# Dealing the TensorE fetch of a three-layer graph attention out in steps, with more columns in it

## The chip, the cores and the metric

The kernel runs on one core of one Trainium2 chip. The metric is the device time of that core in microseconds (us). A core has five engines with a queue of instructions each: PE (TensorE, matmuls; PEld is its loading of weights), DVE (VectorE), ACT (ScalarE), POOL (GpSimd, which issues the indirect DMAs here) and SP (SyncE, which issues plain DMAs).

## What is computed

A graph of 12500 nodes with 32 features each and 400000 directed edges. Three layers of graph attention follow each other, with 2, 2 and 1 heads; then an edge network, whose input and result are put together with a residual and layer norms. One attention layer, cut to what matters:

```python
def _gat(x, edge_index, W, att_s, att_d, bias, heads, ch, neg_slope):
    h = (x @ W.T).reshape(n, heads, ch)
    a_s = (h * att_s[None]).sum(-1)
    a_d = (h * att_d[None]).sum(-1)
    src, dst = (edge_index[0], edge_index[1])
    logits = jax.nn.leaky_relu(a_s[src] + a_d[dst], neg_slope)
    m = jax.ops.segment_max(logits, dst, num_segments=n)
    ex = jnp.exp(logits - m[dst])
    denom = jax.ops.segment_sum(ex, dst, num_segments=n)
    alpha = ex / (denom[dst] + 1e-16)
    out = jax.ops.segment_sum(alpha[:, :, None] * h[src], dst, num_segments=n)
    return out.reshape(n, heads * ch) + bias
```

So every edge needs the row `h[src]` and the number `a_s[src]` of its source node (32 + heads numbers), and then a softmax and a sum over the edges that share a destination. The edge network takes, per edge, the source's row, the destination's row and 32 features of the edge through two small matrices, and takes the maximum over each destination's edges.

## The kernel before

**Tiling.** The edges come sorted by destination. Each of the 128 partitions holds 3125 consecutive edges, one edge per column. A layer walks over the columns in chunks of 60: 50 full chunks and four shorter ones (48, 32, 29 and 16 columns), 54 in all. Layer 2 walks backwards. Sums and maxima over a destination's edges are scans along the columns, with the running values handed from chunk to chunk and at the end from partition to partition. All loops are unrolled, and a scheduler puts each engine's instructions in the order of the program; every engine then works through its own list in order and waits on semaphores for the others.

**Two ways to a source row.** The function `rows_of(c)` allocates a buffer `g` of the pool `gpool` (3 buffers) for a chunk and fills it, column by column. Most columns are filled by a gather: one indirect DMA (L71, issued on POOL) that fetches 128 rows, one for each partition, from the node table in device memory. Every seventh column (`EVERY`, L90; those with t % 7 == 6, so 446 of a layer's 3125, eight or nine of a chunk's 60) is fetched by TensorE instead. For this the whole node table lies in SBUF as `by_group`, three bf16 pieces of each number (so that their sum is the fp32 number), 7 blocks of 14 groups of nodes. `Fetch.fetch` (L244) does, for a chunk: `bm` (L251), a mask on DVE which of the 14 groups a column's nodes are in, for all the chunk's columns at once; then for each column

- `ones_of` spreads the places of the 128 nodes over the partitions with a matmul into PSUM (`places_p`, L255; fp32, two records in the profile), and DVE compares them with the partition numbers (`oh`, L258): seven one-hot matrices of 128x128;
- 21 matmuls (7 blocks, 3 pieces, L270) with these as weights, summed in the PSUM tile `acc` (two buffers);
- DVE multiplies `acc` with `bm` (`mine`, L273) and sums over the 14 groups into the column of `g` (L275).

The one-hot matrix of the next column is made ahead of the matmuls of this one.

**A chunk.** At the head of chunk c the loop of `attention` calls `rows_of(c + 1)`: the gathers and the whole fetch of the next chunk stand in program order ahead of all operations of chunk c. These are then:

- DVE: masks, logits `lg` (up to L804), running maximum (L810), the differences (L815 to L818); ACT: exponentials `wt` (L820), kept in PSUM;
- for each head: ACT `rx` (L830), DVE the rows of `g` times `wt` (`gf`, L833, the last reader of `g`: the second one of a chunk, in layer 3 the only one, frees the buffer), ACT L835, and three scans on DVE (L839; five in layer 3);
- ACT copies `rows` (L842) and SP stores them (L844);
- layers 1 and 2: `finish` divides (`divided`, L586 to L593), applies the activation on ACT (L602 to L604), and in four blocks of up to 16 columns transposes (L615, L617), multiplies with the next layer's weights on PE (L620, L621) and transposes back (L623, L624); layer 3: `finish3` divides, adds the residual (L647) and does a layer norm (L633 to L641);
- SP stores what the next layer reads (L849, L853).

The PSUM tile `fixed` is one bank that holds several things at a time: `places_p`, `small_p` (`wt` and the denominators), biases. Accesses to it from different engines wait for each other.

At the start of layers 2 and 3 `node_groups` builds `by_group` from the layer's node table, with 98 gathers of its own.

In layer 1 every fourth chunk also issues a tenth of the clearing of the table `x_e` (`clear`, from the tile `zeros`) on SP's queue.

## Time and profile before

| what | value |
|---|---|
| median of 10 runs | 22407.24 us (22397.67 to 22432.04) |
| the profiled execution | 22416.65 us, span 22414.9 us |
| mean granted clock of TensorE | 0.696 of full speed |
| busy: PE, PEld, DVE, ACT, POOL | 43%, 20%, 44%, 13%, 50% of the span |
| DMA | 881.63 MB, mean 39 GB/s |
| chain of waits that ended last | "another core or an unknown queue" 34%, DVE 25%, PE 23%, issue 10% |
| attention layer 1 (first to last L842) | about 624 to 6137 us |
| attention layer 2 | about 6573 to 12095 us |
| attention layer 3 | about 12531 to 17508 us |
| edge network | from about 17.5 ms to the end |

The costliest groups of instructions, from the page and the table of lines:

| line | engine | count | busy us | mean ns | idle before, us |
|---|---|---|---|---|---|
| L270 the 21 matmuls of a column | PE | 28098 | 6630.9 | 393 | 671.1 |
| L71 gathers, layer 1 | POOL | 2679 | 2537.6 | 947 | 3181.4, mostly for L833 |
| L71 gathers, layer 2 | POOL | 2679 | 2545.9 | 950 | 3156.8, mostly for L833 |
| L71 gathers, layer 3 | POOL | 2679 | 2542.4 | 949 | 2649.7, mostly for L833 |
| L258 one-hot | DVE | 1338 | 1447.9 | 1082 | 225.1 |
| L273 select | DVE | 1338 | 874.9 | 654 | 5542.2 |
| L275 sum into `g` | DVE | 1338 | 850.0 | 635 | 0.1 |
| L255 spread | PE | 2676 | 666.3 | 337 | 4044.5 |
| L839 scans | DVE | 918 | 757.4 | 869 | 5.5 |
| L833 rows times weights | DVE | 270 | 604.7 | 2240 | 4.0 |

How to read it: busy time is the sum of the durations of a group; "idle before" is how long the engine stood ahead of the group's instructions, which is a wait only if something else waits for that engine. A line is that of the kernel before. Group means mix several shapes where a line has several. "Remote" as the end of a wait names no instruction of this core. A matmul's end is modelled in the profile.

### The profile page before, as it was taken

Reading aid. Unit: us, or ns where it says so; the run is one execution under the profiler, and the core shown is the slowest. Engines: PE = TensorE matmul, PEld = TensorE weight load, DVE = VectorE, ACT = ScalarE, POOL = GpSimd, SP = SyncE. Lnnn points to the kernel's source line nnn. Section 1 sums busy time; section 2 is a strip of 40 time slices with the busy share of each in tenths; the row PEclk is TensorE's granted clock in tenths of the full one; section 3 lists DMA queues with packets and bytes.
Section 4 is the critical chain, followed back from the end, with each engine's and each line's share of the span. In section 5 each row is a group of like instructions: output and inputs, shape, how many; then the busy total and the mean of one; then the engine's idle time right before and its main releaser. Section 6 shows DMA issues by size and latency. Waiting matters only on the chain.

```text
span 22414.9 us, 107898 instructions
## 1 busy us (share of the span) xinstructions
PE 9721.3 (43%) x35914; PEld 4506.4 (20%) x35914; DVE 9825.7 (44%) x13987; ACT 2922.1 (13%) x3898; POOL 11205.9 (50%) x11780
## 2 busy tenths in 40 slices
PE   0545555554534444444443344444444233334332
PEld 0222222222212222222221122222222111111111
DVE  2444444444524444444443344444444445555554
ACT  0111111111101111111111000101001111111111
POOL 6444444444354444444445544445444666666663
PEclk5777777777767777777776676776767666666666
DMA  3111111111101111111111111111111111111111
GB/s 50 45 38 38 49 38 38 40 39 30 34 17 28 28 28 28 30 28 28 28 30 31 31 38 40 42 36 42 38 40 41 45 48 59 55 59 55 59 55 43
DMA packets 562458, 881.63 MB, mean 39 GB/s; under 512 B 267998, under 2 KB 482493, under 8 KB 548445
## 3 DMA queue, kind: packets, MB, share of 16 engines
q1 hardware_dynamic: 185036, 665.01, 8.3%
q0 software_dynamic: 376544, 206.39, 6.4%
q8 instruction: 285, 4.67, 0.1%
q10 hardware_dynamic: 304, 3.20, 0.0%
q14 instruction: 289, 2.37, 0.0%
HBM read 370.51 MB, written 503.27 MB: 39 GB/s over the span
## 4 chain that ended last, share of the span: by engine, by line
another core or an unknown queue 34%; DVE 25%; PE 23%; issue 10%; ACT 4%; POOL 3%; DMA 1%; DVEq 0%; SPq 0%; POOLq 0%; ACTq 0%
PE acc L270 15%; PE ph L981 3%; DVE gf L833 3%; DVE gf L839 3%; DVE oh L258 2%; PE pv L987 1%; DVE yt L617 1%; DVE mine L273 1%; PE ph L620 1%; DVE y L589 1%; PE fixed L255 1%; PE pa L621 1%; DVE y L593 1%; DVE z L908 1%
## 5 line engine op out<-in xcount | busy, mean ns | idle before, releaser
L270 PE MATMUL acc<-by_group,oh 128*128 128x504 bf16 (+2 forms) x28098 | 6630.9, 393 | 671.1 <-issue 663.1
L71 POOL DMA_INDIRECT g<-table,src_i x2679 | 2537.6, 947 | 3181.4 <-DVE gf L833 2355.2
L71 POOL DMA_INDIRECT g<-table,src_last x2679 | 2545.9, 950 | 3156.8 <-DVE gf L833 2355.4
L71 POOL DMA_INDIRECT g<-table,src_first x2679 | 2542.4, 949 | 2649.7 <-DVE gf L833 1847.5
L71 POOL DMA_INDIRECT xs<-table,src_last x3125 | 2985.0, 955 | 1566.1 <-issue 944.2
L270 PEld LDWEIGHTS <-oh 128*128 128x128 bf16 x28098 | 2940.5, 105 | 4070.9 <-issue 1729.8
L273 DVE TENSOR_TENSOR mine<-acc,bm 128x504 f32<-128x504 f32 (+2 forms) x1338 | 874.9, 654 | 5542.2 <-remote 3419.3
L255 PE MATMUL fixed<-ident,fat 128*128 128x128 f32 x2676 | 666.3, 337 | 4044.5 <-DVE oh L258 1493.8
L620 PE MATMUL ph<-yt,w_bd 128*128 128x512 f32 (+2 forms) x840 | 615.0, 824 | 4125.6 <-issue 2793.8
L258 DVE TENSOR_TENSOR oh<-fixed,kid 128x896 bf16<-128x896 f32 x1338 | 1447.9, 1082 | 225.1 <-remote 108.2
L981 PE MATMUL ph<-xt,wb_bd 128*128 128x512 f32 (+2 forms) x832 | 504.4, 693 | 2303.4 <-DVE xt L974 1696.2
L623 DVE STREAM_TRANSPOSE tb<-ph 128x512 f32<-128x512 f32 (+2 forms) x420 | 284.8, 678 | 2704.4 <-remote 2144.7
L255 PEld LDWEIGHTS fixed<-ident,fat 128*128 128x128 f32 x2676 | 554.0, 224 | 4381.8 <-issue 2629.2
L620 PEld LDWEIGHTS ph<-yt,w_bd 128*128 128x128 f32 x840 | 179.8, 250 | 4268.0 <-issue 3809.3
L275 DVE TENSOR_REDUCE g<-mine 128x36 f32<-128x504 f32 (+2 forms) x1338 | 850.0, 635 | 0.1
L987 PE MATMUL pv<-ht,w_bd 128*128 128x512 f32 (+2 forms) x832 | 517.7, 723 | 725.3 <-ACT ht L983 534.0
L820 ACT ACTIVATE fixed<-lg 128x120 f32<-128x120 f32 (+3 forms) x162 | 41.2, 254 | 5636.4 <-DVE oh L258 5635.9
L839 DVE TENSOR_TENSOR_SCAN gf<-rx,gf 128x488 f32<-128x488 f32 (+4 forms) x918 | 757.4, 869 | 5.5
L621 PE MATMUL pa<-yt,a_bd 128*128 128x512 f32 (+2 forms) x840 | 599.0, 805 | 323.5 <-DVE at L624 248.6
L842 ACT COPY rows<-gf 128x2040 f32<-128x2040 f32 (+3 forms) x162 | 628.6, 3880 | 560.4 <-DVE gf L839 560.4
L981 PEld LDWEIGHTS ph<-xt,wb_bd 128*128 128x128 f32 x832 | 187.6, 233 | 2549.1 <-DVE xt L974 1697.3
L625 ACT COPY tb<-at 128x32 f32<-128x32 f32 (+4 forms) x420 | 92.4, 220 | 4468.6 <-DVE at L624 3933.0
(333 smaller groups left out, 10853.1 us busy)
## 6 DMA issues: line engine op xcount, KB each, us to landing
sums<-rows SPq DMA_DIRECT2D x100, 1080.0 KB
table<-tb SPq DMA_DIRECT2D x50, 1020.0 KB
sums<-rows SPq DMA_DIRECT2D x50, 1020.0 KB
x_e<-zeros SPq DMA_DIRECT2D x10, 5000.0 KB
xs<-table,src_last POOLq DMA_INDIRECT x3125
table<-tb SPq DMA_DIRECT2D x50, 990.0 KB
xr<-x_e SPq DMA_DIRECT2D x50, 960.0 KB
table<-xr SPq DMA_DIRECT2D x50, 960.0 KB
```

Of the source, the lines that this page charges most:

```text
L71: return nc.gpsimd.indirect_dma_start(out=dst, out_offset=None, in_=table, in_offset=bass.IndirectOffsetOnAxis(ap=idx, axis=0))
L255: nc.tensor.matmul(places_p, lhsT=bcast(self.at[:, i0 + m:i0 + m + 1], [P, P]), rhs=ident, start=True, stop=True)
L258: nc.vector.tensor_tensor(oh, bcast(places_p[:, None, :], [P, KT, P]), bcast(kid[:, :, None], [P, KT, P]), op=ALU.is_equal)
L270: nc.tensor.matmul(acc, lhsT=oh[:, k, :], rhs=by_group[:, i, k, :KN * w], start=(k == i == 0), stop=(k == KT - 1 and i == 2))
L273: nc.vector.tensor_mul(mine, acc.rearrange("p (w b) -> p w b", b=KN), bcast(bm[:, m:m + 1, :], [P, w, KN]))
L275: nc.vector.tensor_reduce(g[:, t - t0, :w], mine, axis=AX.X, op=ALU.add)
L620: nc.tensor.matmul(ph, lhsT=w_bd, rhs=yt, start=True, stop=True)
L621: nc.tensor.matmul(pa, lhsT=a_bd, rhs=yt, start=True, stop=True)
L833: nc.vector.tensor_mul(v[:, h * wd:h * wd + ch, cur].rearrange("p f t -> p t f"), g[:, :, h * ch:(h + 1) * ch], bcast(wt[:, h, :, None], [ ...
L839: nc.vector.tensor_tensor_scan(turned(gf[:, o:o + k], rev), turned(rx[:, :k], rev), turned(gf[:, o:o + k], rev), 0.0, op0=ALU.mult, op1=AL ...
L981: nc.tensor.matmul(ph, lhsT=wb_bd[:, s, h, :], rhs=x, start=(s == 1), stop=(s == 0))
L987: nc.tensor.matmul(pv, lhsT=w2_bd[:, h, :], rhs=hts[h], start=(h == 0), stop=(h == 1))
```

## The change

`EVERY` becomes 6, 6 and 5 in place of 7, 7 and 7: 520, 520 and 625 columns of a layer are fetched by TensorE, and as many fewer gathered. `Fetch.fetch` becomes `Fetch.columns`, which returns a `Paced` object: a generator that emits one column's instructions at each step, and a rule that spreads the steps evenly over a given number of points. `rows_of(c + 1)` still emits its gathers at the head of chunk c; the columns are emitted at `step()` calls between the operations of chunk c: after the logits, after `wt`, after L835 and after the scans of each head, and in `finish` after the activation and in each block after the matmuls (11 points in a full chunk of layers 1 and 2, for 10 columns and 11 steps), in `finish3` at five places (9 points in layer 3, for 12 columns and 13 steps). What is left is emitted at the head of the next chunk (`rest`). Within the fetch the select of a column (L273, L275) now comes after the matmuls of the next. The mask `bm` has room for 12 columns in place of 9, and the tile `zeros`, from which `clear` writes, has 250 numbers per partition in place of 500, with more and smaller packets for the same bytes.

```diff
--- before.py
+++ after.py
@@ -87,7 +87,7 @@
 
-    EVERY = {1: 7, 2: 7, 3: 7}
+    EVERY = {1: 6, 2: 6, 3: 5}
...
@@ -146,7 +146,7 @@
-    zeros = const.tile([P, 500], F32, name="zeros")
+    zeros = const.tile([P, 250], F32, name="zeros")
...
@@ -218,6 +218,29 @@
+    class Paced:
+
+
+        def __init__(self, steps, count):
+            self.steps, self.count, self.taken, self.passed = steps, count, 0, 0
+
+        def at_points(self, points):
+            self.points = points
+            return self
+
+        def __call__(self):
+            self.passed += 1
+            while self.taken < min(self.count, -(-self.count * self.passed // self.points)):
+                next(self.steps)
+                self.taken += 1
+
+        def rest(self):
+            for _ in self.steps:
+                pass
+
+    def alone():
+        pass
+
     class Fetch:
 
 
@@ -241,15 +264,14 @@
         def __contains__(self, t):
             return bool(self.every) and t < TE // self.every * self.every and t % self.every == self.every - 1
 
-        def fetch(self, psum, g, t0, n, bufs=2):
+        def columns(self, psum, g, t0, n):
+
+
 
             todo = [t for t in range(t0, t0 + n) if t in self]
             if not todo:
-                return
+                return Paced(iter(()), 0)
             pool, w, i0 = self.pool, self.w, todo[0] // self.every
-            bm = pool.tile([P, 9, KN], F32, name="bm")[:, :len(todo), :]
-            nc.vector.tensor_tensor(bm, bcast(count[:, None, :KN], [P, len(todo), KN]),
-                                    bcast(self.b[:, i0:i0 + len(todo), None], [P, len(todo), KN]), op=ALU.is_equal)
 
             def ones_of(m):
                 nc.tensor.matmul(places_p, lhsT=bcast(self.at[:, i0 + m:i0 + m + 1], [P, P]), rhs=ident,
@@ -259,20 +281,32 @@
                                         bcast(kid[:, :, None], [P, KT, P]), op=ALU.is_equal)
                 return oh
 
-            coming = ones_of(0)
-            for m, t in enumerate(todo):
-                oh = coming
-                if m + 1 < len(todo):
-                    coming = ones_of(m + 1)
-                acc = psum.tile([P, 512], F32, name="acc", bufs=bufs)[:, :KN * w]
-                for k in range(KT):
-                    for i in range(3):
-                        nc.tensor.matmul(acc, lhsT=oh[:, k, :], rhs=by_group[:, i, k, :KN * w],
-                                         start=(k == i == 0), stop=(k == KT - 1 and i == 2))
+            def select(m, acc, bm):
                 mine = pool.tile([P, D + 4, KN], F32, name="mine")[:, :w, :]
                 nc.vector.tensor_mul(mine, acc.rearrange("p (w b) -> p w b", b=KN),
                                      bcast(bm[:, m:m + 1, :], [P, w, KN]))
-                nc.vector.tensor_reduce(g[:, t - t0, :w], mine, axis=AX.X, op=ALU.add)
+                nc.vector.tensor_reduce(g[:, todo[m] - t0, :w], mine, axis=AX.X, op=ALU.add)
+
+            def steps():
+                bm = pool.tile([P, 12, KN], F32, name="bm")[:, :len(todo), :]
+                nc.vector.tensor_tensor(bm, bcast(count[:, None, :KN], [P, len(todo), KN]),
+                                        bcast(self.b[:, i0:i0 + len(todo), None], [P, len(todo), KN]), op=ALU.is_equal)
+                oh, acc = ones_of(0), None
+                for m in range(len(todo)):
+                    coming = ones_of(m + 1) if m + 1 < len(todo) else None
+                    done, acc = acc, psum.tile([P, 512], F32, name="acc", bufs=2)[:, :KN * w]
+                    for k in range(KT):
+                        for i in range(3):
+                            nc.tensor.matmul(acc, lhsT=oh[:, k, :], rhs=by_group[:, i, k, :KN * w],
+                                             start=(k == i == 0), stop=(k == KT - 1 and i == 2))
+                    if m:
+                        select(m - 1, done, bm)
+                    oh = coming
+                    yield
+                select(len(todo) - 1, acc, bm)
+                yield
+
+            return Paced(steps(), len(todo) + 1)
 
     def node_groups(li, idx, w):
 
@@ -298,7 +332,7 @@
     def clear(table, part=0, parts=1):
...
         k = TE * table.shape[1] // parts
-        z = next(z for z in range(500, 0, -1) if k % z == 0)
+        z = next(z for z in range(250, 0, -1) if k % z == 0)
...
@@ -592,7 +626,7 @@
         bias = b_all[:, 2, :] if li == 3 else biases[li]
         nc.vector.tensor_add(y, y, bcast(bias[:, :, None], [P, D, n]))
 
-    def finish(li, pool, psum, den, v, n):
+    def finish(li, pool, psum, den, v, n, step=alone):
 
         y = pool.tile([P, D * T], F32, name="y", bufs=1)[:, :D * n].rearrange("p (f t) -> p f t", t=n)
         divided(li, y, den, v, n)
@@ -602,6 +636,7 @@
         nc.scalar.activation(e, y, AF.Relu, scale=down)
         nc.scalar.activation(y, y, AF.Relu, scale=up)
         nc.scalar.activation(e, e, AF.Exp, scale=-1.0)
+        step()
         heads = HEADS[li + 1]
         w_bd, a_bd = weights[li + 1]
         tb = pool.tile([P, T, D + heads], F32, name="tb")[:, :n, :]
@@ -619,6 +654,7 @@
             pa = psum.tile([P, TB * D], F32, name="pa")[:, :w]
             nc.tensor.matmul(ph, lhsT=w_bd, rhs=yt, start=True, stop=True)
             nc.tensor.matmul(pa, lhsT=a_bd, rhs=yt, start=True, stop=True)
+            step()
             at = pool.tile([P, TB, D], F32, name="at", bufs=1)[:, :nt, :]
             nc.vector.transpose(tb[:, b:b + nt, :D], blocks(ph))
             nc.vector.transpose(at, blocks(pa))
@@ -626,26 +662,31 @@
             nc.scalar.copy(ta[:, b:b + nt, :], at[:, :, heads:2 * heads])
         return tb, ta
 
-    def layernorm(lp, st, x, n, sq=None):
+    def layernorm(lp, st, x, n, sq=None, step=alone):
         st = st[:, :n]
         if sq is None:
             sq = lp.tile([P, T, D], F32, name="sq", bufs=1)[:, :n, :]
         nc.vector.tensor_reduce(st, x, axis=AX.X, op=ALU.add)
         nc.vector.tensor_scalar(st, st, 1.0 / D, None, op0=ALU.mult)
+        step()
         nc.vector.tensor_sub(x, x, bcast(st[:, :, None], [P, n, D]))
         nc.scalar.activation(sq, x, AF.Square)
+        step()
         nc.vector.tensor_reduce(st, sq, axis=AX.X, op=ALU.add)
         nc.vector.tensor_scalar(st, st, 1.0 / D, EPS, op0=ALU.mult, op1=ALU.add)
         nc.scalar.activation(st, st, AF.Sqrt)
+        step()
         nc.vector.reciprocal(st, st)
         nc.vector.tensor_mul(x, x, bcast(st[:, :, None], [P, n, D]))
 
-    def finish3(pool, psum, den, v, x, n):
+    def finish3(pool, psum, den, v, x, n, step=alone):
 
         y = psum.tile([P, D * 64], F32, name="y3")[:, :D * n].rearrange("p (f t) -> p f t", t=n)
         divided(3, y, den, v, n)
+        step()
         nc.vector.tensor_add(x, x, y.rearrange("p f t -> p t f"))
-        layernorm(pool, den[:, T:], x, n)
+        step()
+        layernorm(pool, den[:, T:], x, n, step=step)
 
     def empties():
 
@@ -763,15 +804,17 @@
                     for t in range(n):
                         if t0 + t not in fetch:
                             gather(g[:, t, :], table, idx[:, t0 + t:t0 + t + 1])
-                    fetch.fetch(psp, g, t0, n)
-                    return g
+                    return g, fetch.columns(psp, g, t0, n)
 
                 old = None
                 coming = rows_of(0)
                 for c, (t0, n) in enumerate(todo):
-                    g = coming
+                    g, step = coming
+                    step.rest()
+                    step = alone
                     if c + 1 < len(todo):
                         coming = rows_of(c + 1)
+                        step = coming[1].at_points(2 + 2 * heads + (1 + -(-n // TB) if li < 3 else 5))
                     (ad, xr) = loaded
                     if c + 1 < len(todo):
                         loaded = load(c + 1)
@@ -802,6 +845,7 @@
                                                      0.0 if c == 0 else old[1][:, h:h + 1], op0=ALU.mult, op1=ALU.add)
                         nc.vector.tensor_add(lg[:, h, :], g[:, :, D + h], af[:, h, :])
                     nc.vector.scalar_tensor_tensor(lg, lg, slope, lg, op0=ALU.mult, op1=ALU.max)
+                    step()
                     if c == 0:
                         nc.vector.memset(mx[:, :, carry:carry + 1], 0.0)
                     else:
@@ -818,6 +862,7 @@
                     nc.vector.tensor_sub(lg, lg, mx[:, :, cur])
                     wt = small_p[:, :heads * n].rearrange("p (h t) -> p h t", t=n)
                     nc.scalar.activation(wt, lg, AF.Exp)
+                    step()
 
                     gf = sp.tile([P, gw * (T + 1)], F32, name="gf")
                     v = gf[:, :gw * (n + 1)].rearrange("p (f t) -> p f t", t=n + 1)
@@ -833,11 +878,13 @@
                         nc.vector.tensor_mul(v[:, h * wd:h * wd + ch, cur].rearrange("p f t -> p t f"),
                                              g[:, :, h * ch:(h + 1) * ch], bcast(wt[:, h, :, None], [P, n, ch]))
                         nc.scalar.copy(v[:, h * wd + ch, cur], wt[:, h, :])
+                        step()
                         for f in range(0, wd, FS):
                             k = min(FS, wd - f) * (n + 1)
                             o = (h * wd + f) * (n + 1)
                             nc.vector.tensor_tensor_scan(turned(gf[:, o:o + k], rev), turned(rx[:, :k], rev),
                                                          turned(gf[:, o:o + k], rev), 0.0, op0=ALU.mult, op1=ALU.add)
+                        step()
                     rows = sp.tile([P, T, gw + heads], F32, name="rows", bufs=1)[:, :n, :]
                     nc.scalar.copy(rows[:, :, :gw], v[:, :, cur].rearrange("p f t -> p t f"))
                     nc.scalar.copy(rows[:, :, gw:], mx[:, :, cur].rearrange("p h t -> p t h"))
@@ -845,10 +892,10 @@
                     e = 0 if rev else n - 1
                     old = (v[:, :, done:done + 1], af[:, :, e], mx[:, :, done:done + 1])
                     if li < 3:
-                        tb, ta = finish(li, fp, fps, den, v[:, :, cur], n)
+                        tb, ta = finish(li, fp, fps, den, v[:, :, cur], n, step)
                         nc.sync.dma_start(out=edge_rows(gives[li + 1])[:, t0:t0 + n, :], in_=ta)
                     else:
-                        finish3(fp, fps, den, v[:, :, cur], xr, n)
+                        finish3(fp, fps, den, v[:, :, cur], xr, n, step)
                         tb = xr
                     nc.sync.dma_start(out=edge_rows(tables[li + 1])[:, t0:t0 + n, :], in_=tb)
 
```

## The prediction

> **What bounds the kernel now.** I read the page first (PE 43%, DVE 44%, POOL 50% busy: no engine is full, so something takes turns), then the timeline of one steady chunk, then the table of windows, and last the start of layer 2. In the timeline of a steady chunk of layer 1 the gathers on POOL start when the second L833 of a chunk has freed a buffer of `g`, run at one per 1.25 us, and then POOL waits:
>
> ```profile
> 3039.76 0.94 POOL L71 DMA_INDIRECT g<-table,src_i  x1 [44.26 <-DVE gf L833]
> 3041.01 0.95 POOL L71 DMA_INDIRECT g<-table,src_i  x1 [0.31 <-issue]
> ...
> 3103.56 0.94 POOL L71 DMA_INDIRECT g<-table,src_i  x1 [0.30 <-issue]
> 3151.62 0.95 POOL L71 DMA_INDIRECT g<-table,src_i  x1 [47.12 <-DVE gf L833]
> ```
>
> So POOL is done long before it may go on; the gathers run three chunks ahead and nobody waits for their rows. The period, 3039.76 to 3151.62, is 111.9 us. The table of windows cuts it, and one of layer 3, and the start of layer 2 (columns: us, then busy us and count of PE matmuls, weight loads, DVE, ACT, POOL; granted clock, DMA share, GB/s):
>
> ```profile
> 3039.76:3111.97 72.21, 18.71 (x47) 7.32 (x48) 22.79 (x45) 14.03 (x15) 49.19 (x52) 0.62 0.14 30
> 3111.97:3151.62 39.65, 39.44 (x176) 18.98 (x176) 25.59 (x33) 1.36 (x7) 0.00 (x0) 0.96 0.07 29
> 14027.99:14099.05 71.06, 15.56 (x60) 7.04 (x58) 26.95 (x39) 9.28 (x7) 49.23 (x52) 0.62 0.21 56
> 14099.05:14131.24 32.19, 31.05 (x149) 16.22 (x150) 18.61 (x22) 0.43 (x2) 0.00 (x1) 0.89 0.00 1
> 6355.02:6483.81 128.79, 20.33 (x46) 5.90 (x46) 5.21 (x11) 0.00 (x0) 98.60 (x100) 0.53 0.10 14
> 6527.61:6566.95 39.34, 37.82 (x196) 19.84 (x195) 24.37 (x43) 1.88 (x5) 0.00 (x0) 1.00 0.01 3
> ```
>
> A chunk has two phases. While gathers run (and some 7 us after the last) PE gets through 47 or 60 matmuls in 71 to 72 us. When they are over it does 176 in 39.65 us, without a gap (39.44 busy). The fifth row says that this is no lack of work: at the start of layer 2 gathers run without a break and fetched columns are all that PE and DVE have, and two columns (46 matmuls and 46 weight loads) take 128.79 us, 64.4 each. Without gathers (sixth row) a column takes 4.38 us. DVE shows who waits there, and PE that it crawls at one matmul per 2.80 us:
>
> ```profile
> 6412.67 0.65 DVE L273 TENSOR_TENSOR mine<-acc,bm 128x476 f32<-128x476 f32 x1 [56.53 <-remote]
> 6477.07 0.65 DVE L273 TENSOR_TENSOR mine<-acc,bm 128x476 f32<-128x476 f32 x1 [57.15 <-issue]
> 6383.25 0.56 PE L270 MATMUL acc<-by_group,oh 128*128 128x476 bf16 x1 [2.25 <-issue]
> 6386.05 0.55 PE L270 MATMUL acc<-by_group,oh 128*128 128x476 bf16 x1 [2.24 <-issue]
> ```
>
> 92 PE instructions in 128.79 us is one per 1.40 us, which was also the spacing of the gathers there: about one PE instruction per gather. Why, no view tells; I take it as a fact of this trace. So gathers and fetch hardly overlap: the period is their sum.
>
> By the timeline, periods depend on both parts: with 51 gathers and 8 columns 107.4 us, with 51 and 9 111.0, with 52 and 9 112.1 (medians, layers 1 and 2); in layer 3 97.6, 100.9, 102.8. Means: 110.1 (layers 1 and 2), 100.3 (layer 3).
>
> **Removed and added.** Columns per layer go from 446 to 520, 520 and 625; a full chunk has 10, 10 and 12 in place of 8.57, and 50, 50 and 48 gathers in place of 51.43. Each column adds 23 matmuls (21 at L270, 2 at L255) and 2.4 us of DVE (L258 1.08, L273 0.65, L275 0.64), and takes one gather of 1.25 us off POOL.
>
> *Layers 1 and 2.* The gather phase of the first row has 52 gathers; 50 make it 72.21 - 2x1.25 = 69.7 us, in which PE does 47 - 2 = 45 matmuls. A chunk has 10x23 + 16 (in `finish`) = 246; 201 are left, at 39.65/176 = 0.225 us: 45.3. Period 115.0 us if the dealing itself is worth nothing.
>
> *Layer 3.* 71.06 - 4x1.25 = 66.1 us with 60 - 4 = 56 matmuls; 12x23 - 56 = 220 left at 32.19/149 = 0.216: 47.5. Period 113.6.
>
> **Moved: what the dealing gains.** Now a chunk's whole fetch ends before L820 of the chunk before it, and PE is idle from the end of the last column (3039.24) to 3049.03, when L593 lets the next L255 at `fixed`. After the change columns are due at just that time, and early in a gather phase PE is not yet slow: in the edge network 32 matmuls passed in the first 16 us beside gathers without a late semaphore; in the chunk above, 21 begun 12 us after the first gather took 18 us, in layer 3, begun after 28 us, 39.5. Bounds per chunk: 0, and 9.8/0.225 = 43 matmuls (layer 3: as many as it does in the whole phase now, 60). I take 20, nearest to the chunk's own row: -4.5 us in layers 1 and 2, -4.3 in layer 3.
>
> **Moved: what the dealing costs.** DVE runs in program order. Now its operations on a chunk (48.4 us less 9 columns: 26.8; layer 3 45.6 - 21.1 = 24.5) mostly lie in the gather phase, where nothing else can go on: free. After, a `step` in their midst puts an L258 that waits for an L255 queued behind 21 slow matmuls ahead of them. With two or three columns dealt past the start of the gathers, DVE stands there for the rest of the phase; queued behind it in layers 1 and 2 are the four blocks of `finish` (L615, L617, L623, L624: 3.1 us each), the small operations up to L818 (4.3) and, of the next chunk, L833 (3.9) and three L839 (2.4); ACT waits for DVE, SP's stores for ACT, and POOL for L833. In layer 3 it is `divided` (5.0), L647, the layernorm (11.6 with L647), and L833 (3.8). All this comes after the gathers, beside PE. If every hand-over fits, PE stays the longer one (45 us against 36 to 40 of DVE) and the cost is 0; if each operation makes PE wait (L255 must wait for every earlier reader of the bank `fixed`: L833, L587, L593, L633 to L641), it is some 12 us in layers 1 and 2 and 20 in layer 3. I take 4 and 6, nearer to 0, since steps and operations are of like length (4.7 us of PE against 2.4 + 2.3 of DVE).
>
> Covers: the larger `bm` is one 0.3 us DVE operation per chunk; `zeros` of 250 makes ten x_e clears of twice as many packets on SP's queue (15 us of traffic each now, with nothing waiting; 0, and if the cover is gone at most 150 us in all). At a layer's start there are fewer gathers (150 for 154 at 1.40 us), and only one chunk's columns must end before the first chunk (some 5 fewer at 4.4 us, given back in part): 0 to -35 us, I take -15 for each of three.
>
> **The sum.** Layers 1 and 2: 115.0 - 4.5 + 4 = 114.5, +4.4 us on 110.1, for 98 full periods: +431. Layer 3: 113.6 - 4.3 + 6 = 115.3, +15.0 on 100.3, for 49: +735. Starts -45. Together +1121 us on the profiled 22416.65 (span 22414.9): 23538; the median lies 9.4 below that execution: 23530 us.
>
> The Trainium skill, "SBUF — State Buffer", section "Who interferes with whom", states the contrary: PE waits on no one, and DMA does not contend with a compute engine. By it the columns would cost 4.4 us beside gathers too, POOL's 62.6 us would set the period, and the estimate would be the second rival below; the 64.4 us per column measured here decide against it.
>
> **Rivals.**
> - *Early columns (faster).* PE's idle time after the first gather is filled with 43 matmuls (layer 3: 60) and DVE's operations find room: periods 115.0 - 9.7 = 105.3 and 113.6 - 13.0 = 100.6; 98x(-4.8) + 49x0.3 - 105 = -560: about 21850 us. For it: PE's idle 9.8 us, and the 32 matmuls of the edge network. Against: the slow column begun 12 us after the first gather. It decides from 35 matmuls per chunk, net of new waits: 98x4.9 + 49x13.3 = 1132 us against 98x0.225 + 49x0.216 = 32.6 us per matmul.
> - *PE is free (much faster).* The slowness comes from the lump of columns, not from the gathers; dealt out it goes, and POOL sets the period: 50x1.25 = 62.6 and 48x1.25 = 60.0. 98x(-47.5) + 49x(-40.3): about 15800 us. Against: the start of layer 2.
> - *Dealing does nothing.* The order that the engines get is nearly the old one, since L255 must wait for the bank anyway; only the extra columns count, 115.0 and 113.6: 98x4.9 + 49x13.3 - 45 = +1087, about 23490 us.
> - *Strict turns.* All waits are paid: 122.5 and 129.3; 98x12.4 + 49x29.0 - 45: about 25000 us.
>
> **Chances.** Slower with the dealing worth little either way (forecast and third rival) 0.59, strict turns 0.06, early columns 0.27 (its point of decision, 35, lies between the 20 that I took and the bound of 43; a fifth of it within 0.2%, about what a measurement of this kernel tells from no change), PE free 0.08 with all that lies between. Faster 0.30, same 0.05, slower 0.65. The range, 21700 to 24600, leaves out PE free, the strongest early columns and most of the strict turns, together some 0.2.
>
> **What would show it.** Right: L270 x34965; gathers x2605, x2605 and x2500; still one pause of POOL per chunk, of 45 to 55 us, ended by L833; in windows of a gather phase 50 to 80 matmuls, in the rest PE busy over 85%; PE at work within 3 us of the first gather; L258, not L273, as the line before which DVE stands in that phase; periods near 114.5 and 115. Wrong: POOL without a pause, columns of 5 us beside gathers after the first 16 us, or a rest phase of under 40 us.

## The result, and the profile after

The changed kernel takes 23532.18 us (median of 8 runs, 23517.06 to 23543.18), the kernel before beside it 22409.14 us: 1.0501 times as long, with a 95% interval of 1.0492 to 1.051. The forecast was 23530 us, slower.

The profiled execution of after took 23480.55 us (span 23478.8), 52 us less than the median; that of before 22416.65. So the traces have 1064 of the 1123 us between them. The instruction starts in the two traces put the spans 1066 us apart; they divide it as follows (a period runs from the last reader of `g` in one chunk to that in the next):

| stretch | before, us | after, us | difference |
|---|---|---|---|
| layer 1, the 49 periods from the first chunk on | 5336.4 (108.9 each) | 5413.3 (110.5) | +76.9 |
| layer 2, the same | 5349.0 (109.2) | 5521.2 (112.7) | +172.2 |
| layer 3, the same | 4852.4 (99.0) | 5643.2 (115.2) | +790.8 |
| the short chunks at the three ends | 487.9 | 553.8 | +65.9 |
| starts of the three layers | | | -52.1 |
| from the last chunk of layer 3 to the end | 4896.6 | 4908.7 | +12.1 |

First the timeline of POOL in the changed kernel (start, us busy, engine, line, operation, and in brackets the idle time before it and what ended it), at the beginning and end of one steady chunk's gathers in layer 1, and the first of the next:

```profile
3055.05 0.95 POOL L71 DMA_INDIRECT g<-table,src_i  x1 [52.92 <-DVE gf L878]
...
3116.33 0.95 POOL L71 DMA_INDIRECT g<-table,src_i  x1 [0.30 <-issue]
3170.62 0.95 POOL L71 DMA_INDIRECT g<-table,src_i  x1 [53.34 <-DVE gf L878]
```

One phase of gathers at 1.25 us each and one pause, ended by the last reader of `g` (L878, formerly L833), as before: nothing of the sequence has been dissolved, only its two parts have other lengths. The table of windows shows them, cut as before (us, then busy us and count of PE matmuls, weight loads, DVE, ACT, POOL; granted clock, DMA share, GB/s): the gather phase and the rest in layer 1, the same in layer 3, the start of layer 2, and the first 12 us of the first gather phase:

```profile
3055.05:3123.33 68.28, 15.40 (x71) 7.18 (x69) 13.53 (x18) 10.28 (x6) 47.29 (x50) 0.63 0.14 30
3123.33:3170.62 47.29, 42.90 (x177) 20.04 (x177) 36.51 (x62) 5.29 (x17) 0.00 (x0) 0.92 0.07 25
15063.04:15128.84 65.80, 21.12 (x90) 9.15 (x90) 16.49 (x20) 3.97 (x2) 45.42 (x48) 0.64 0.13 28
15128.84:15178.90 50.06, 40.65 (x186) 20.55 (x186) 36.60 (x49) 5.87 (x8) 0.00 (x1) 0.87 0.11 40
6421.75:6550.55 128.80, 20.29 (x46) 5.88 (x46) 5.21 (x10) 0.00 (x0) 98.61 (x100) 0.53 0.10 14
3055.05:3067.05 12.00, 12.00 (x60) 5.91 (x59) 10.20 (x15) 4.11 (x2) 9.25 (x10) 1.00 0.33 107
```

The last row is what the dealing brought: 60 matmuls beside the first ten gathers, with PE never idle, where before PE stood still. The first row is what it did not bring: in the 56 us after those 12 there were only 11 more. So the standstill beside gathers is there with dealt columns as with a lump. The fifth row is that of before to 0.01 us (128.80 against 128.79, 46 matmuls): at a layer's start the first chunk's columns still come together.

The timeline of DVE (the first fence) and that of PE (the second) show where they stand in these two chunks, with the idle time in brackets:

```profile
3124.03 1.09 DVE L280 TENSOR_TENSOR oh<-fixed,kid 128x896 bf16<-128x896 f32 x1 [47.11 <-remote]
15118.68 0.64 DVE L286 TENSOR_TENSOR mine<-acc,bm 128x462 f32<-128x462 f32 x1 [38.99 <-remote]
15129.88 1.09 DVE L280 TENSOR_TENSOR oh<-fixed,kid 128x896 bf16<-128x896 f32 x1 [8.48 <-remote]
```

```profile
3076.39 0.80 PE L277 MATMUL fixed<-ident,fat 128*128 128x128 f32 x2 [7.58 <-issue]
3125.18 0.80 PE L277 MATMUL fixed<-ident,fat 128*128 128x128 f32 x2 [47.15 <-DVE oh L280]
15159.55 0.80 PE L277 MATMUL fixed<-ident,fat 128*128 128x128 f32 x2 [4.55 <-DVE xr L680]
```

In layer 1 DVE stands 47.11 us before the one-hot of the next column (L280, formerly L258), and all that the chunk still has for DVE stands behind it. In layer 3 it stands before the select (L286) first, and then before L280. Both engines stand in that time: L280 reads the places that L277 writes, by the first line of PE that L277 was over at 3077.19, DVE starts at 3124.03, and PE, by its second line, waits those 47.15 us for DVE. So there PE isn't short of time; the word that L277 is done reaches DVE 47 us late. (The trace's record of PE's semaphore agrees: the update that lets L280 go is at 3124.01. Away from gathers such an update comes some 0.02 us after the end of the instruction.) The last line of PE is a hand-over that the dealing added: the places of the next column go into the bank `fixed`, which the layer norm is still using, and PE waits 4.55 us for it.

### The profile page after: what moved, and what is told of

Read it like the earlier page. It is cut to its first block, busy times and chain, and to the rows that moved or that the text cites. A ratio compares the mean times of both kernels' runs of the same rounds, so it can differ in the third digit from the quotient of the medians.

```text
span 23478.8 us, 124110 instructions
## 1 busy us (share of the span) xinstructions
PE 10950.4 (47%) x43435; PEld 5141.1 (22%) x43435; DVE 10576.6 (45%) x14968; ACT 2949.3 (13%) x3898; POOL 10884.7 (46%) x11453
## 5 line engine op out<-in xcount | busy, mean ns | idle before, releaser
L300 PE MATMUL acc<-by_group,oh 128*128 128x462 bf16 (+2 forms) x34965 | 8098.4, 388 | 1011.1 <-issue 924.9
L300 PEld LDWEIGHTS <-oh 128*128 128x128 bf16 x34965 | 3593.7, 103 | 4997.3 <-issue 1964.2
L277 PE MATMUL fixed<-ident,fat 128*128 128x128 f32 x3330 | 846.1, 341 | 7740.7 <-DVE oh L280 5776.7
L286 DVE TENSOR_TENSOR mine<-acc,bm 128x462 f32<-128x462 f32 (+2 forms) x1665 | 1082.9, 650 | 6528.3 <-remote 4621.4
L280 DVE TENSOR_TENSOR oh<-fixed,kid 128x896 bf16<-128x896 f32 x1665 | 1805.1, 1084 | 2958.2 <-remote 2413.1
L277 PEld LDWEIGHTS fixed<-ident,fat 128*128 128x128 f32 x3330 | 638.1, 216 | 8270.4 <-DVE oh L280 5955.9
L288 DVE TENSOR_REDUCE g<-mine 128x33 f32<-128x462 f32 (+2 forms) x1665 | 1063.3, 639 | 3.6
L648 ACT ACTIVATE pe<-e,minus 128x512 f32<-128x512 f32 (+2 forms) x420 | 278.1, 662 | 5279.1 <-DVE yb L650 5265.3
L1035 DVE STREAM_TRANSPOSE vf<-pv 128x512 f32<-128x512 f32 x208 | 226.3, 1088 | 853.9 <-remote 384.6
L878 DVE TENSOR_TENSOR gf<-g,fixed 128x960 f32<-128x960 f32 (+5 forms) x270 | 604.4, 2239 | 1.6 <-ACT fixed L864 1.2
L655 PE MATMUL ph<-yt,w_bd 128*128 128x512 f32 (+2 forms) x840 | 435.5, 601 | 223.6 <-DVE yt L652 90.7
L1030 ACT ACTIVATE ht<-ph,b_c 128x512 f32<-128x512 f32 (+2 forms) x416 | 271.4, 661 | 2018.0 <-remote 1025.2
```

The source lines that it names most:

```text
L277: nc.tensor.matmul(places_p, lhsT=bcast(self.at[:, i0 + m:i0 + m + 1], [P, P]), rhs=ident, start=True, stop=True)
L280: nc.vector.tensor_tensor(oh, bcast(places_p[:, None, :], [P, KT, P]), bcast(kid[:, :, None], [P, KT, P]), op=ALU.is_equal)
L286: nc.vector.tensor_mul(mine, acc.rearrange("p (w b) -> p w b", b=KN), bcast(bm[:, m:m + 1, :], [P, w, KN]))
L288: nc.vector.tensor_reduce(g[:, todo[m] - t0, :w], mine, axis=AX.X, op=ALU.add)
L300: nc.tensor.matmul(acc, lhsT=oh[:, k, :], rhs=by_group[:, i, k, :KN * w], start=(k == i == 0), stop=(k == KT - 1 and i == 2))
L655: nc.tensor.matmul(ph, lhsT=w_bd, rhs=yt, start=True, stop=True)
```

## Experiments

The times of before were 22409 us beside the changed kernel, 22189 us beside the first four runs below, and 22415 to 22452 us beside the others: chips differ by 1%. So ratios are those to the kernel before on the same chip, and periods of different groups are compared only where the difference is larger than that.

**1. The dealing alone, the columns alone, and fewer columns.** Four kernels ask which part of the change costs the time, and whether a column costs more than the gather that it saves.

Dealing alone:

```diff
 (in the changed kernel)
-    EVERY = {1: 6, 2: 6, 3: 5}
+    EVERY = {1: 7, 2: 7, 3: 7}
```

> The changed kernel with every seventh column fetched by TensorE again (446 columns per layer); only the dealing is left of the change. Theory S (gathers and columns add up, a matmul outside the gathers costs 0.225 us in layers 1 and 2 and 0.216 in layer 3): the trace of the changed kernel shows 81, 70 and 90 matmuls done beside the gathers. With 213, 213 and 197 of a chunk, 132, 143 and 107 are left; with the 3 to 6 us of hand-overs read there, periods near 105, 107 and 103 us against 108.9, 109.2 and 99.0 before: 49x(-3.9-2.2+4.0), some 100 us faster, with the starts 22300 (22150 to 22550). Rival D (the loss comes from the dealing: an L258 that waits in the midst of a chunk's operations): over 23000 us.

Measured: 22234.92 us, 1.0023 times before (1.0013 to 1.0032). Rival D is out: the dealing is not the loss. The gain of 100 us was not there either. The periods were 105.6, 105.6 and 103.0 us, but the chip was a faster one, so only layer 3 is clear: 103.0 against 99.0 is a loss of 4 us or more.

Columns alone:

```diff
 (in the kernel before; bm for 12 columns and zeros of 250 as in the change)
-    EVERY = {1: 7, 2: 7, 3: 7}
+    EVERY = {1: 6, 2: 6, 3: 5}
```

> The kernel before with the change's numbers of columns (520, 520 and 625 per layer) and tile sizes; the fetch stays one lump ahead of a chunk's operations. Theory S: 33 matmuls more per chunk in layers 1 and 2 and 79 more in layer 3 come after the gathers, less 1.43 and 3.43 gathers of 1.25 us: +4.9 and +13.3 us per chunk, 98x4.9 + 49x13.3 = 1132 us, 23540 (23350 to 23750). Rival D: the columns cost nothing beside the gathers, under 22600 us.

Measured: 23262.47 us, 1.0483 times before (1.0465 to 1.05); theory S had 23540 on 22409, 1.0505. So the columns alone (with the larger `bm` and the halved zeros) make nearly the whole loss: 1.0483 against the 1.0501 of the change, and the two intervals overlap.

No columns:

```diff
 (in the kernel before)
-    EVERY = {1: 7, 2: 7, 3: 7}
+    EVERY = {1: 0, 2: 0, 3: 0}
```

> The kernel before without any column fetched by TensorE: all 3125 columns of a layer are gathered, and the node groups of layers 2 and 3 are not built. Theory S: POOL sets the period, 60 gathers at 1.25 to 1.40 us are 75 to 84 us against 108.9, 109.2 and 99.0; PE has 16 matmuls per chunk (none in layer 3) which fit beside them. 49x(3x79.5 - 317.1) = -3850 us, and some 0.4 ms less at the starts of layers 2 and 3: 18000 (17300 to 19000). Rival G (the gathers are what a chunk waits for and a column relieves them, so 60 of them take longer than 51 gathers and the columns): over 22400 us.

Measured: 18522.79 us, 0.8346 times before (0.8332 to 0.836). Rival G is out by far, and the 446 columns of before were already a loss, by the periods alone and not only by the node groups that are not built. The table of lines of this run (busy us, mean ns of one, idle before them) shows POOL at work throughout, with hardly a wait that another engine ends:

```profile
L71 POOL DMA_INDIRECT g<-table,src_first x3125 | 3336.3, 1068 | 1011.7 <-issue 996.4 <-DMA g<-table,src_first 15.2
```

The periods are 81.4, 83.8 and 83.6 us for 60 gathers, 1.36 to 1.40 us each: gathers that go on without a break come no faster than that on average, though a phase of 51 runs at 1.25.

Few columns:

```diff
 (in the kernel before)
-    EVERY = {1: 7, 2: 7, 3: 7}
+    EVERY = {1: 20, 2: 20, 3: 20}
```

> The kernel before with every twentieth column fetched by TensorE (156 per layer, 3 of a chunk). Theory S: 57 gathers are 71.3 us, with 9.2 us around them 80.5, in which 47 to 60 of 69 + 16 matmuls are done; 25 to 38 are left, 6 to 9 us: periods of 82 to 90 us, 49x(3x86 - 317.1) = -2900 us: 19500 (18800 to 20200), between the kernel without columns and the kernel before. Rival G: slower than before.

Measured: 20130.55 us, 0.9067 times before (0.9033 to 0.91), between none and every seventh as theory S had it, but dearer than it said: on 22409 us its range is 0.839 to 0.901, and that the time lies inside the range is owed to the faster chip. Periods were 93.8, 93.3 and 85.9 us where 82 to 90 were expected; in layers 1 and 2 only 45 and 49 matmuls passed beside the gathers, the lower end of the 47 to 60.

**2. Where the dealing gains and loses, and how PE crawls.** The next four ran on one chip, the first of them the kernel before for its profile.

> The kernel before, for a profile on the same chip as the next three runs: the median of the kernel before was 22409 us beside the changed kernel and 22189 us beside the first four experiments, so periods of different calls can be 1% apart. Periods within 1% of 108.9, 109.2 and 99.0 us.

Measured: periods of 109.0, 109.0 and 99.1 us, 22432.65 us.

Dealing in layers 1 and 2 only:

```diff
 (in the changed kernel with EVERY 7, 7, 7)
-    step = coming[1].at_points(2 + 2 * heads + (1 + -(-n // TB) if li < 3 else 5))
+    if li < 3:
+        step = coming[1].at_points(2 + 2 * heads + 1 + -(-n // TB))
+    else:
+        coming[1].rest()
```

> The changed kernel with every seventh column fetched by TensorE, dealt out in layers 1 and 2 only; in layer 3 the whole fetch stands ahead of the chunk's operations again. If the dealing gains where a gather phase now starts with PE at work, and loses in layer 3 where the layer norm is in its way (105.6, 105.6 and 103.0 us in the first experiment): 2 to 3.5 us less per period of layers 1 and 2, none in layer 3: 0.985 to 0.991 of the kernel before. Rival: the three layers of the first experiment look different only because the chips do, and the dealing is worth nothing anywhere: 0.998 to 1.003.

Measured: 22326.53 us, 0.9947 times before (0.9934 to 0.9961). The sign is that of the first case and the size falls short of it: 108.1 and 107.9 us against 109.0 and 109.0, and 99.2 against 99.1 in layer 3, so one us per period. The dealing gains a little in layers 1 and 2 (98 periods, some 100 us), and loses more in layer 3 (49 periods of 4 us or more): a small loss, as experiment 1 had it, though its 0.2% is less than these two figures would give.

Matmuls split in two:

```diff
 (in Fetch.fetch of the kernel before)
-    nc.tensor.matmul(acc, lhsT=oh[:, k, :], rhs=by_group[:, i, k, :KN * w], ...)
+    for f0, f1 in ((0, KN * 16), (KN * 16, KN * w)):
+        nc.tensor.matmul(acc[:, f0:f1], lhsT=oh[:, k, :], rhs=by_group[:, i, k, f0:f1], ...)
```

> The kernel before with each of the 21 matmuls of a column split in two of half the width (224 and 252, 252 or 280 numbers), the same sums. Theory I (beside gathers PE's pace is one per instruction): as many matmuls beside the gathers as before, 45 to 60, though each does half as much. Theory W (the pace is one of data read or written): twice as many, 85 to 120. In both the period is longer, since a chunk has 393 matmuls: I 115 to 135 us, W 105 to 120.

Measured: periods of 115.9, 113.9 and 101.9 us (23195.62 in all), and 65, 62 and 80 matmuls in a gather phase where the run of before on this chip had 47, 47 and 58. That is 1.35 times as many, between the two theories and nearer to I. It doesn't decide.

Gathers further apart:

```diff
 (in rows_of of the kernel before; zeros of 250, and a tile spare of 128x250)
     gather(g[:, t, :], table, idx[:, t0 + t:t0 + t + 1])
+    for v in range(4):
+        nc.gpsimd.memset(spare, float(v))
```

> The kernel before with four memsets of 128x250 numbers on POOL after each gather of a layer (some 0.3 us each by the row of the 128x256 memset), so that gathers stand 2.4 to 2.6 us apart; the tile that clears are written from is halved as in the change. A gather phase becomes some 135 us. Theory T (PE gets one instruction through per gather, however far apart they are): still 45 to 60 matmuls beside the gathers, then 35 us or more: periods near 170, some 31500 us. Theory H (PE stands only while a gather is being put out): all 213 matmuls pass beside the gathers, periods of 130 to 140, under 27500. Theory R (PE has a lower rate as long as gathers go on, by time): some 90 matmuls beside them, rest 28 us, periods near 162.

Measured: 26077.9 us, but the edit didn't do what it says. Nothing kept the memsets in their places: the scheduler put some 60 of them in a row ahead of a chunk's first gather, and one was left behind each gather. The rest stood ahead of the node groups and of the edge network, where the time went (3746 memsets, 1154 us, between layers 1 and 2 alone). In the attention layers, though, the periods were 96.9, 93.9 and 103.7 us: layers 1 and 2 were shorter than before, with more work on POOL. The timeline of DVE in a gather phase and the windows around it say why:

```profile
3035.18 0.68 DVE L274 TENSOR_TENSOR mine<-acc,bm 128x504 f32<-128x504 f32 x1 [2.42 <-PE acc L271]
3039.86 0.68 DVE L274 TENSOR_TENSOR mine<-acc,bm 128x504 f32<-128x504 f32 x1 [2.42 <-PE acc L271]
```

```profile
3029.00:3041.00 12.00, 12.00 (x61) 6.15 (x60) 5.67 (x8) 0.00 (x0) 10.69 (x17) 1.00 0.11 14
3041.00:3053.00 12.00, 12.00 (x59) 5.73 (x58) 9.13 (x11) 0.48 (x2) 10.69 (x18) 1.00 0.11 12
```

A column every 4.68 us, PE busy in 24.00 of 24 us at a clock of 1.00, with gathers going on all the time, one per 1.44 us. The three theories had all been about how PE shares time with gathers. None of them had PE at full pace beside gathers that stand only 0.19 us further apart. These 24 us lie within the first 36 us of a gather phase, and then the phase's columns are done.

**3. What of it frees PE.** One memset, held at its place, and then the smallest one:

```diff
 (in rows_of of the kernel before; the first with zeros of 250)
     gather(g[:, t, :], table, idx[:, t0 + t:t0 + t + 1])
+    tc.keep_in_program_order(nc.gpsimd.memset(spare, 0.0))     # spare: 128x250, then 128x8
```

> The kernel before with one memset of 128x250 numbers on POOL behind each gather of a layer, held at its place; zeros halved as in the change. In the run with four memsets, most of them had run ahead of the gathers; in the stretches where one was left behind each gather, gathers stood 1.44 us apart, PE was busy without a gap and columns took 4.7 us. Theory K (PE crawls only beside gathers with nothing between them on POOL): POOL sets the period, 51.4x1.44 = 74 us, with up to 8 us of waits 74 to 82: 49x(3x78 - 317.1) = -4070 us on 22452, 18400 (17500 to 19000). Theory L (there the crawl was over because POOL was late by 22 us of memsets each chunk, not because of the one between): periods of 109 or more, over 22400 us.

Measured: 17946.97 us, 0.8002 times before (0.7989 to 0.8015), the fastest of all. Theory K holds in that POOL sets the period, with periods of 76.1, 78.3 and 78.1 us. The halved zeros are not the reason: the columns alone had them too, at 1.0483. POOL's timeline, a window over one of its rounds, and DVE's selects late in that round:

```profile
3099.62 0.95 POOL L71 DMA_INDIRECT g<-table,src_i  x1 [0.17 <-issue]
3100.58 0.32 POOL L767 MEMSET spare<- 128x250 f32 x1
3101.06 0.95 POOL L71 DMA_INDIRECT g<-table,src_i  x1 [0.16 <-issue]
...
3127.68 0.95 POOL L71 DMA_INDIRECT g<-table,src_i  x1 [6.62 <-DVE gf L835]
```

```profile
3127.68:3202.00 74.32, 47.67 (x200) 22.17 (x200) 50.15 (x81) 17.36 (x23) 65.93 (x103) 0.88 0.19 44
```

```profile
3164.26 0.68 DVE L274 TENSOR_TENSOR mine<-acc,bm 128x504 f32<-128x504 f32 x1 [4.04 <-PE fixed L256]
3171.54 0.68 DVE L274 TENSOR_TENSOR mine<-acc,bm 128x504 f32<-128x504 f32 x1 [4.17 <-remote]
3178.69 0.68 DVE L274 TENSOR_TENSOR mine<-acc,bm 128x504 f32<-128x504 f32 x1 [4.07 <-remote]
```

200 matmuls in 74.32 us full of gathers; before, it was 47 in 72.21. POOL's pause, 44 to 47 us in the chunk of before, is 6.62 here. PE is not wholly free, though: some 36 us into the round a column takes 7.2 us in place of 4.68, with the gathers still 1.44 us apart, and in the middle of the three layers the median from one select to the next is 7.2 to 7.9 us.

> The kernel before with one memset of 128x8 numbers behind each gather, held at its place: the shortest instruction, so the gathers stand little further apart than without it (1.25 us) and closer than the 1.40 us at which PE crawled at the start of layer 2. If any instruction between two gathers is enough: POOL sets the period, 51.4x1.2 to 1.3 = 62 to 67 us, with waits 64 to 75: 17000 (16300 to 18000). If PE needs the pause of 0.3 us and more that the larger memset gives: no gain, 22300 to 22700.

Measured: 22135.13 us, 0.9871 times before (0.9854 to 0.9887). An instruction between two gathers is not enough by itself:

```profile
3129.50 0.95 POOL L71 DMA_INDIRECT g<-table,src_i  x1 [0.18 <-issue]
3130.45 0.12 POOL L767 MEMSET spare<- 128x8 f32 x1
3130.76 0.95 POOL L71 DMA_INDIRECT g<-table,src_i  x1 [0.18 <-issue]
```

The gathers stand 1.26 us apart for the first 25 or so of a phase. Then memsets wait, some for the memset before them, and gathers come 1.26 to 2.6 us apart, 1.37 to 1.38 us on the average of a phase. 67, 68 and 86 matmuls pass in a phase, more than the 47, 47 and 58 of before and far fewer than a chunk's 213.

**4. The change with a pause between gathers.** The changed kernel, and its numbers of columns in one lump, each with

```diff
     gather(g[:, t, :], table, idx[:, t0 + t:t0 + t + 1])
+    for v in range(2):
+        tc.keep_in_program_order(nc.gpsimd.memset(spare, float(v)))     # spare: 128x48
```

> The changed kernel with two memsets of 128x48 numbers on POOL behind each gather of a layer, each held at its place (0.15 us each by the rows of 128x8, 0.12, and 128x250, 0.32; with the pauses of 0.05 and 0.16 around them, gathers 1.47 us apart). If the pause is what PE needs: 50 gathers are 73.5 us and 48 are 70.6, PE's 246 and 276 matmuls at 0.20 to 0.225 us are 49 to 62 and fit; with the 2 to 5 us of waits of the run with the memset of 250, periods of 76, 76 and 74 us against 76.1, 78.3 and 78.1 there: 17700 (17300 to 18200). If the dealing makes DVE wait also where PE is free: periods of 80 and more, over 18200. If it is the size of the memset that counts and not the pause: near 23500.

Measured: 23125.37 us, 1.0309 times before (1.0292 to 1.0327).

> The change's numbers of columns in one lump, with the same two memsets behind each gather. If the pause frees PE and the order of the fetch then does not matter, as POOL sets the period: within 1% of the changed kernel with the two memsets, 17700 (17300 to 18200). If the dealing is worth something once PE is free: that kernel is over 1% faster; if it costs: this one.

Measured: 23102.72 us, 1.0297 times before (1.028 to 1.0315).

Both missed, because the pause wasn't made. POOL's timeline of the first has one memset behind a gather, and the second ones in a row after the last:

```profile
3001.11 0.95 POOL L71 DMA_INDIRECT g<-table,src_i  x1 [0.16 <-issue]
3002.06 0.15 POOL L809 MEMSET spare<- 128x48 f32 x1
3002.37 0.95 POOL L71 DMA_INDIRECT g<-table,src_i  x1 [0.16 <-issue]
...
3038.97 9.12 POOL L809 MEMSET spare<- 128x48 f32 x47 [0.70 <-POOL spare L809]
3080.83 0.95 POOL L71 DMA_INDIRECT g<-table,src_i  x1 [32.74 <-DVE gf L881]
```

The gathers stood 1.27 us apart for the first 30 or so of a phase, and 1.36 to 1.38 on its average. So the pair says nothing on the change under gathers 1.44 us apart, and whether more columns or the dealing pay there stays open. It says two other things. Such a spacing is too close, like that of the run before. And dealt or in one lump, the same columns take the same time in all (23125 and 23103 us on one chip), but not layer by layer: dealt, the periods are 111.4, 107.7 and 112.1 us, in one lump 112.9, 111.1 and 106.2. The dealing gains 1.5 and 3.4 us a period in layers 1 and 2 and loses 5.9 in layer 3, and that the two cancel is a chance of this kernel.

## Why the prediction was right

**The mechanism.** Gathers and fetch follow each other; a further column costs 23 matmuls of 0.22 us after the gathers and saves 1.25 us of gathers. Experiment 1 shows this from both sides: 520 and 625 columns 1.0483, 446 columns 1, 156 columns 0.9067, none 0.8346. The decisive rows were the start of layer 2 and the two windows of one chunk. The "PE is free" rival, by which the lump of columns makes the slowness, is refuted by the dealt gather phase: 11 matmuls in its last 56 us, with PE and DVE both standing until the gathers are over; and with the columns still in one lump, a memset behind each gather took the standstill away.

Two readings behind the mechanism were wrong, though the sum didn't need them. The gathers at the start of layer 2 stood 1.25 us apart up to 6439.67 and 1.40 only from 6440.95 on, so PE's pace of one instruction per 1.40 us did not follow their spacing, and "about one PE instruction per gather" holds for the counts of the window alone (92 and 100). And the "18 us" and "39.5" that 21 matmuls are said to take are the times from their start to DVE's select of the sum (3070.20 and 14096.25). By PE's own rows they took 7.30 us (from 3052.02) and 6.99 us (from 14056.46): in these two chunks it is not PE's work that comes late but the word of it.

**The terms.** For the chunks in the middle of a layer, matmuls and times counted from the trace of after as in the prediction, as means (what lies between the gather phases is all "rest"; gain and hand-overs are worked out from the counts):

| | layer 1 | layer 2 | layer 3 |
|---|---|---|---|
| gather phase, forecast and measured, us | 69.7, 68.3 | 69.7, 68.3 | 66.1, 65.8 |
| matmuls in it, forecast (with the 20 of the dealing) and measured | 65, 81 | 65, 70 | 76, 90 |
| dealing's gain, forecast and from the counts, us | 4.5, 8.1 | 4.5, 5.6 | 4.3, 7.3 |
| rest, forecast and measured, us | 44.8, 42.9 | 44.8, 45.0 | 49.2, 50.2 |
| of it hand-overs, forecast and what is left over, us | 4, 5.8 | 4, 5.4 | 6, 10.0 |

(Gain: (81 - 45) x 0.225 = 8.1, and so on; layer 3 (90 - 56) x 0.216. Hand-overs: 42.9 - (246 - 81) x 0.225 = 5.8, 45.0 - 176 x 0.225 = 5.4, 50.2 - 186 x 0.216 = 10.0.) Both terms of the dealing were sized too small, by up to a factor of two, and they offset each other: the step that failed is the choice of 20 matmuls, "nearest to the chunk's own row", and of its rows the one of 18 us was the misread one. Early in a phase PE works at full pace (60 in 12 us), so in layer 1 the 9.8 us in which it stood were filled nearly whole, 36 of the bound of 43; in layers 2 and 3, with 25 of 43 and 34 of 60, the truth lies nearer to the 20. In layer 1 the gain is the larger, in layer 3 the hand-overs, of which the line with L680 is one.

**The sum.** Forecast were +431 for layers 1 and 2, +735 for layer 3 and -45 for the starts; measured +249, +791 and -52, and with the short chunks, for which the forecast had nothing, +66, and +12 at the end. Layers 1 and 2 were 182 us too dear and layer 3 with the short ends 122 too cheap; the profiled execution of after lies 52 us under its median. That the total is right to 2 us is an accident of these; its size to a few hundred is not.

**Rivals.** "Dealing does nothing" (23490 us) was 42 us off, and for the whole it describes the result as well as the forecast: 1.0501 dealt and 1.0483 in one lump, 1.0309 and 1.0297 with the memsets, 1.0023 at every seventh. Its reason, that the engines get nearly the old order, is not what the layers show: the dealing gains in layers 1 and 2 and loses in layer 3. "Early columns" had the filling of PE's idle time right (36, 25 and 34 matmuls) but not that hand-overs take most of it back, in layer 3 more than all of it; its point of decision, 35, was meant net of them. "Strict turns" was not reached: 5.4 to 10 us of its 12 and 20.

**The signs forecast.** The counts (34965, 2605, 2605, 2500), one pause of POOL ended by the last reader of `g` (48 to 54 us in layer 1; 56 in layer 3, just over the 45 to 55), PE busy in 90.7% of the rest in layer 1 (42.90 of 47.29), PE at work from the first gather on (12.00 of the first 12 us) and the wait before L258 in layer 1 came as said. In layer 3 PE was busy in 81% (40.65 of 50.06) where 85% was said, DVE waited longer before the select than before L258, the matmuls of a phase were 81 in layer 1 and 90 in layer 3 where 80 was the limit, and layer 1's period was 110.5 us and not 114.5.

**A page against the trace.** The Trainium skill, "SBUF — State Buffer", section "Who interferes with whom", says that PE waits on no one and DMA does not contend with an engine. For the time of a kernel, the rows contradict it beside gathers in close order (64.4 us per column at the start of layer 2); beside gathers 1.44 us apart they agree for some 36 us of a round (4.68 us per column) and less after that (7.2). The section is about the ports of SBUF, and no run here shows that what delays PE lies there. It was right to let the row decide; the prediction took the row as a fact about gathers, though, when it was one about gathers in close order.

## What to carry to other kernels

Price an operation from a row where it runs beside the same neighbours: a column was 4.4 us alone and 64.4 us beside the gathers, and everything followed from that. When an engine crawls beside another that is issuing as fast as it can, try to slow the other one a little before work is moved from one to the other: here 0.19 us more per gather took 20% off the time, and leaving the moved work out 16.5%. Where a filler instruction landed must be read in the timeline before its time means anything; here neither four loose memsets nor two pinned ones stayed where they were written. And before an engine is called slow, compare when its instruction ended with when the next engine took the result: here 47 us lay between the two.

## What the runs showed of the chip

- Beside gathers issued 1.25 us apart, what PE has done reaches DVE late after the first 12 us or so of a phase: 47 us late in the chunk shown. Over a whole run, a one-hot of DVE starts more than 20 us after the end of the matmul that it reads about once per chunk: 160 times in before, 157 in after.
- Gathers 1.26 or 1.27 us apart for the first 25 or 30 of a phase (1.36 to 1.38 on its average) do no better: 158, 162 and 160 times in the three runs with the smaller memsets. In the two runs with gathers 1.44 us apart it is 6 times and 4, though a column still takes 7.2 us late in a round, in place of 4.68. Nothing was run between.
- Gathers without a break take 1.36 to 1.40 us each (no columns; the start of layer 2 from 6440.95 on), while a phase of 51 is issued at 1.25. A reading that fits some of this: gathers are worked off at about 1.40 us, POOL at 1.25 runs ahead of that, and PE has to take turns while the backlog stands. It would grow to 51 x 0.15 = 7.7 us in a phase, about the 7 us for which PE and DVE stand on after the last gather. It would not arise at 1.44, though, where columns are slowed late in a round all the same. This is argued from the numbers; what PE and gathers share, and whether PE is slowed or its signals, has not been shown. The halved matmuls leave open whether the turns go by instructions or by data.
